# One attention stream over all pairs of heads, chain ends emitted a step later, and query maxima entered as rows by DMA

## The chip, the core and the metric

One core of a Trainium2 chip runs the whole program in one launch. The metric is device time in microseconds (us), the median of several executions. The engines named below are TensorE (PE in the profile; PEld is its weight load), VectorE (DVE), ScalarE (ACT), GpSimd (POOL) and the SP queue that issues most DMAs. Everything is float32.

## What is computed

The input is 16 images of 192 channels and 32x32 positions. Four residual layers follow, each `x = x + f(groupnorm(x))`; the change lies in layers 1 to 3.

```python
# layer 0: a recurrent block (mLSTM) plus a 3x3 convolution and batch norm over all images
# layer 1: 6 heads, 1024 tokens each; q and k (4 numbers a token) come from a small quantum circuit
scores = -(qn + kn - 2.0 * qk) / tau            # qk: product over 4 numbers
out = softmax(scores, axis=-1) @ v              # v: 32 channels of the head
# layer 2: deformable 3x3 depthwise convolution, 4 corners gathered for each tap
off = conv3x3(x, w_off) + b_off
acc = sum over 9 taps, 4 corners of gather(x, corner) * weight * w_def
# layer 3: 1x1 convolution, 2x2 Fourier weights, depthwise 3x3, gelu gate, 1x1 convolution
```

## The kernel before

`circuits` and `phase_a` (layer 0) come first and are not touched. `phase_b` runs layers 1 to 3 as four streams of Python generators, each going through the 16 images: `vectors` (layer 0's batch norm, x1, the group norm, the circuit's q and k), `attention`, `layer2` (`layer2_offsets`, then `layer2_gathers`) and `layer3`. Each `yield` names a cost; `weave` always goes on with the stream whose summed cost, divided by the stream's total for an image and shifted by its offset, is least. So one unit of `weave` is one image in each stream, and the offsets say how many images later a stream starts: 0, 1.1, 2.2, 3.5. The order so emitted is the order of preference in which the framework fills each engine's queue; an instruction whose inputs or buffer aren't there can be overtaken when that queue is laid out[...].

PSUM has eight banks: `big` (two buffers of two banks: `pmax`, `pscore`, `paug`, `pcirc`, `phad`), `mm` (two buffers of one bank: `pgn`, `pgv`, `pqub`, `ppsi`, `pz`, `pzt`, `pv`, `pxt`, `poffc`, `poff`, `pdt`, `pout`), `pav` and `pdef` (one each).

In `attention` heads go in pairs, three to an image. `largest(pr)` transposes the queries and keys of the pair (`rows_of`), makes all scores in 16 `pmax` products of 128 tokens by 512 keys for two heads, and takes their maxima on VectorE (L1139) into `mx`; the negative maximum then becomes column 5 of the query table `qp`. `values(pr)` transposes `qp` again with the maxima in it, and for each half of the tokens makes eight score products (`pscore`, L1160), each with an exponential on ScalarE (L1163), and their products with V (`pav`, L1170), two at a time right after the two exponentials. The sums are then copied, inverted by Ln and Exp (L1180, L1181) and multiplied (L1182). Between the steps of `values(pr)` stand those of `largest(pr + 1)`; `largest(0)` of an image stands alone, and the last pair has no maxima beside it.

In `layer2_gathers` a tap takes two gathers of 128 rows (L1311), corner 0 on ScalarE (L1298), three corners on VectorE (L1300), the tap's weight (L1316) and a product with the identity that sums taps in `pdef` (L1317); after nine taps the block is copied (`df`), transposed, added and stored. `layer3` ends with `pout` products, each followed at once by its addition and its store.

Of the kernel before, what the change touches and what calls it, by code (L numbers as in the profile page):

```python
# [19 lines left out]
HW = 1024  # L20
HS = 512


def groupstats(nc, pool, mm, cn, x):

    st = pool.tile([96, 2, 2, 6], F32, tag="gnst", name="gnst")
    mv = pool.tile([96, 2, 2], F32, tag="gnmv", name="gnmv")
    for k in range(2):
        for h in range(2):
            nc.vector.bn_stats(st[:, k, h, :], x[k][:, h * HS:(h + 1) * HS])  # L30
        nc.vector.bn_aggr(mv[:, k, :], st[:, k, :, :].rearrange("p a b -> p (a b)"))
    pg = mm("pgn")
    nc.tensor.matmul(pg[:96, 0:2], cn.g6, mv[:, :, 0], start=True, stop=True)
    gm = pool.tile([96, 2], F32, tag="gngm", name="gngm")
    nc.vector.tensor_copy(gm, pg[:96, 0:2])
    dd = pool.tile([96, 2], F32, tag="gndd", name="gndd")
    nc.vector.tensor_sub(dd, mv[:, :, 0], gm)
    nc.vector.tensor_mul(dd, dd, dd)
    nc.vector.tensor_add(dd, dd, mv[:, :, 1])
    pv = mm("pgv")  # L40
    nc.tensor.matmul(pv[:96, 0:2], cn.g6, dd, start=True, stop=True)
    rs = pool.tile([96, 2], F32, tag="gnrs", name="gnrs")
    nc.scalar.activation(rs, pv[:96, 0:2], AF.Ln, bias=cn.eps5[:96])
    nc.scalar.activation(rs, rs, AF.Exp, scale=-0.5)
    return gm, rs


def groupnorm(nc, pool, mm, cn, x, out):

    gm, rs = groupstats(nc, pool, mm, cn, x)  # L50
    nm = pool.tile([96, 2], F32, tag="gnnm", name="gnnm")
    nc.vector.scalar_tensor_tensor(nm, gm, -1.0, rs, ALU.mult, ALU.mult)
    for k in range(2):
# [718 lines left out]
def phase_b(tc, d, out, ydram, stats, cn, nb):  # L772

    nc = tc.nc
    with ExitStack() as ctx:
# [24 lines left out]
        def pairs(name):  # L800
            return p2.tile([128, 2, 192], F32, tag="acc", name=name, bufs=4)
# [97 lines left out]
        vo = p1.tile([128, 8, 3, 96], F32, name="vo")  # L899
        nc.vector.memset(vo[:, :, :, 32:64], 1.0)  # L900


        qp_, kp_, kt_, qt_ = [], [], [], []
        for i in range(2):
            for name, into, n in (("qp", qp_, 560), ("kp", kp_, 560), ("kt", kt_, HW), ("qt", qt_, HW)):
                if name == "kp" and i:
                    continue
                t = p1.tile([128, n], F32, name=f"{name}{i}")
                nc.gpsimd.memset(t, 0.0)
                into.append(t.rearrange("p (t c) -> p t c", t=8) if n == 560 else t)  # L910
# [10 lines left out]
        xnd = dp.tile([nb, 192, HW], F32, name="xnd")  # L921
        x1d, x2d, x3d = (dp.tile([nb, 192, HW], F32, name=f"x{i}d") for i in range(1, 4))
# [9 lines left out]
        def stream(i, work):  # L932
            for b in range(nb):
# [7 lines left out]
        weave([(stream(0, vectors), 86.0), (stream(1, attention), 189.6, 1.1), (stream(2, layer2), 144.5, 2.2),  # L941
               (stream(3, layer3), 121.4, 3.5)])


def vectors(g, b, left):
# [17 lines left out]
    groupnorm(nc, p2, mm, cn, x, xn)  # L963
    yield 8.0
# [52 lines left out]
    for pr in range(3):  # L1017
# [5 lines left out]
        psi = psi.rearrange("p t h a b -> p t (h a b)")  # L1023
# [7 lines left out]
        yield 4.0  # L1031
        prob = {}
        for w in range(2):
            for hf in range(2):
# [5 lines left out]
                prob[w, hf] = v4("prob")  # L1040
                nc.scalar.activation(prob[w, hf], pc, AF.Square)  # L1041
            yield 4.0

        pz = mm("pz")
        for hh in range(2):
            o = 20 - (pr * 2 + hh) * 4
            for w in range(2):
                for hf in range(2):
                    q = (w * 2 + hf) * 32
                    nc.tensor.matmul(pz[q:q + 32, :], g.amat[:, w, o:o + 32], prob[w, hf][:, hh * HS:(hh + 1) * HS],  # L1050
                                     start=(hh == 0), stop=(hh == 1))
# [4 lines left out]
        yield 4.0  # L1056
# [31 lines left out]
def attention(g, b, left):  # L1088

    nc, cn, p2 = g.nc, g.cn, g.p2  # L1090
    big, e4, row = g.big, g.e4, g.row
    qk, kr, vo = left.qk, left.kr, g.vo


    xn = [g.v4("xn")[:96] for _ in range(2)]
    for k in range(2):
        nc.sync.dma_start(xn[k], g.xnd[b, k * 96:k * 96 + 96, :])
    for t2 in range(4):
        pv = g.mm("pv")
        for j in range(2):  # L1100
            tt = t2 * 2 + j
            for k in range(2):
                nc.tensor.transpose(pv[:, (j * 2 + k) * 96:(j * 2 + k) * 96 + 96],
                                    xn[k][:, tt * 128:(tt + 1) * 128], cn.ident[:96, :96])
        for o in range(2):
            nc.scalar.activation(vo[:, t2 * 2:t2 * 2 + 2, :, o * 64:o * 64 + 32].rearrange("p a h e -> p (a h) e"),
                                 pv[:, 0:384].rearrange("p (a o e) -> p a o e", o=2, e=32)[:, :, o, :], AF.Copy,
                                 scale=row("gate"))
    yield 3.0
# [7 lines left out]
    def largest(pr):  # L1117

        qp, kp, kT, qT = g.qp_[pr % 2], g.kp_[0], g.kt_[pr % 2], g.qt_[0]
        for hh in range(2):  # L1120
            h, o = pr * 2 + hh, hh * 64
            nc.vector.tensor_copy(qp[:, :, o:o + 4], qk[:, :, 0, h, :])
            nc.vector.memset(qp[:, :, o + 4:o + 5], 1.0)
            nc.vector.memset(qp[:, :, o + 5:o + 6], 0.0)
            nc.vector.tensor_scalar_mul(kp[:, :, o:o + 4], qk[:, :, 1, h, :], g.rtau[:, 0:1])
            nc.vector.tensor_copy(kp[:, :, o + 4], kr[:, :, h])
            nc.vector.memset(kp[:, :, o + 5:o + 6], 1.0)
        rows_of(kp, kT)
        rows_of(qp, qT)
        yield 5.0  # L1130
        mx = p2.tile([128, 8, 2, 2], F32, tag="mx", name="mx")
        for tt in range(8):
            for hf in range(2):
                pm = big("pmax").rearrange("p (h s) -> p h s", h=2)
                for hh in range(2):
# [5 lines left out]
        nc.vector.tensor_tensor(qp.rearrange("p t c -> p c t")[:, 5::64, :].rearrange("p h t -> p t h"),  # L1141
                                mx[:, :, 0, :], mx[:, :, 1, :], ALU.min)

    att = g.xtile("att")

    def values(pr):

        kT, qT = g.kt_[pr % 2], g.qt_[1]
        rows_of(g.qp_[pr % 2], qT)
        for hf in range(2):  # L1150
            s = slice(hf * HS, (hf + 1) * HS)
            po = g.ps("pav")
            for t2 in range(4):
                pe = []
                for j in range(2):
                    tt = t2 * 2 + j
                    ps = big("pscore")
                    for hh in range(2):
                        r = slice(hh * 64, hh * 64 + 64)
                        nc.tensor.matmul(ps[:, hh * HS:(hh + 1) * HS], kT[r, tt * 128:(tt + 1) * 128], qT[r, s],  # L1160
                                         start=True, stop=True)
                    pe.append(e4("pexp"))
                    nc.scalar.activation(pe[j], ps, AF.Exp)  # L1163
                    if j == 0:
                        yield 1.2
                for j in range(2):
                    tt = t2 * 2 + j
                    for hh in range(2):

                        nc.tensor.matmul(po[hh * 64:hh * 64 + 64], vo[:, tt, pr, hh * 32:hh * 32 + 64],  # L1170
                                         pe[j][:, hh * HS:(hh + 1) * HS], start=(tt == 0), stop=(tt == 7))
                yield 3.3

            pc = p2.tile([128, HS], F32, tag="pavc", name="pavc", bufs=1)
            nc.scalar.activation(pc, po, AF.Identity)
            rd = p2.tile([128, HS], F32, tag="rd", name="rd", bufs=1)
            for hh in range(2):
                h = pr * 2 + hh
                num, den = (slice(0, 32), slice(32, 64)) if hh == 0 else (slice(96, 128), slice(64, 96))
                nc.scalar.activation(rd[num, :], pc[den], AF.Ln)  # L1180
                nc.scalar.activation(rd[num, :], rd[num, :], AF.Exp, scale=-1.0)  # L1181
                nc.vector.tensor_tensor(att[(h % 3) * 32:(h % 3) * 32 + 32, h // 3, s], pc[num], rd[num, :], ALU.mult)  # L1182
# [3 lines left out]
    for pr in range(3):  # L1186
        ahead = largest(pr + 1) if pr < 2 else iter(())
        for cost in values(pr):
            yield cost
            yield next(ahead, 0.0)  # L1190
        for cost in ahead:
            yield cost
    for k in range(2):
        x1 = g.v4("x1")[:96]
        nc.sync.dma_start(x1, g.x1d[b, k * 96:k * 96 + 96, :])
        nc.vector.tensor_add(att[:, k, :], att[:, k, :], x1)
        nc.sync.dma_start(g.x2d[b, k * 96:k * 96 + 96, :], att[:, k, :])
        yield 3.0
    left.x = att


def layer2(g, b, left):
    yield from layer2_offsets(g, b, left)
    yield from layer2_gathers(g, b, left)


def layer2_offsets(g, b, left):
# [5 lines left out]
    groupnorm(nc, p2, mm, cn, [x[:, k, :] for k in range(2)],  # L1213
              [xpad[:, k, 1:33, 1:33] for k in range(2)])
    yield 5.0
# [72 lines left out]
def layer2_gathers(g, b, left):  # L1288
# [3 lines left out]
    xg, ix, w4 = g.xg[b % 2], left.ix, left.w4  # L1292

    def corner(cr, part):
        for acc, j, gt, c in part:
            a, v, w = acc[:, j, :], gt[:, cr * 192:(cr + 1) * 192], w4[:, cr, c:c + 1]
            if cr == 0:
                nc.scalar.activation(a, v, AF.Copy, scale=w)  # L1298
            else:
                nc.vector.scalar_tensor_tensor(a, v, w, a, ALU.mult, ALU.add)  # L1300

    for hf in range(2):
        for j2 in range(2):
            po = g.ps("pdef")
            for t in range(9):
                part = []
# [290 lines left out]
```

## Time and profile before

| | us |
|---|---|
| median of 3 runs | 9228.33 |
| lowest and highest | 9214.2, 9228.97 |
| the profiled execution | 9226.07 |
| its span, first to last instruction | 9224.3 |

| engine | busy us | share | instructions |
|---|---|---|---|
| PE | 7894.4 | 86% | 30720 |
| DVE | 6946.3 | 75% | 14595 |
| ACT | 4251.9 | 46% | 7414 |
| POOL | 1882.9 | 20% | 1681 |

The mean granted TensorE clock is 0.909. A busy time counts instructions from start to end, waits not included. `phase_b` starts near 3332 us; from 4048 to 8481 all four streams run at once.

### The profile page before, as it was taken

To read this page: it belongs to the slowest core of one execution; us is meant where nothing else is said; L and a number is where in the kernel's file an instruction comes from. 1 tells how busy PE (TensorE), PEld (TensorE's weight loads), DVE (VectorE), ACT (ScalarE), POOL (GpSimd) and SP (SyncE) were. 2 spreads that over 40 slices of the span, in tenths; PEclk is the share of its full clock that TensorE was granted. 3 is DMA by queue.
4 is the path that set the end of the run, shared out by engine and by line. 5 is a ranking of instruction groups with operands and counts; after the bars stand their busy time and mean duration, and the time that the engine had idled before them with its cause. 6 is when DMAs were issued, how large, how long until landed. Compare 5 with 4: busy or idle time off the path is not lost. (4 is left out here: it accounts for less than half of the span.)

```text
span 9224.3 us, 92174 instructions
## 1 busy us (share of the span) xinstructions
PE 7894.4 (86%) x30720; PEld 3453.5 (37%) x30720; DVE 6946.3 (75%) x14595; ACT 4251.9 (46%) x7414; POOL 1882.9 (20%) x1681
## 2 busy tenths in 40 slices
PE   5999999999999969888888888888888888888853
PEld 2555555555555532233233233233233333333221
DVE  7777777777777743678878778878878878877887
ACT  3444444444454424444545545444544545445432
POOL 0100100100100100222312412322312322223341
PEclk9899999999999979998988998988988988989976
DMA  1111111111111120433433433433433333333341
GB/s 53 43 43 42 48 48 43 45 43 42 49 46 43 42 53 24 135 114 114 138 104 117 128 113 119 126 112 115 126 107 114 122 120 116 116 121 112 121 151 61
DMA packets 299050, 813.72 MB, mean 88 GB/s; under 512 B 46459, under 2 KB 162493, under 8 KB 298571
## 3 DMA queue, kind: packets, MB, share of 16 engines
q0 software_dynamic: 92160, 453.06, 15.9%
q1 hardware_dynamic: 206411, 354.76, 12.5%
q8 instruction: 241, 3.95, 0.2%
q14 instruction: 238, 1.95, 0.1%
HBM read 666.74 MB, written 132.54 MB: 87 GB/s over the span
## 5 line engine op out<-in xcount | busy, mean ns | idle before, releaser
L1311 POOL DMA_INDIRECT gt<-xg,ix x1152 | 1561.6, 1356 | 4173.2 <-DVE w L1283 1963.1
L1137 PE MATMUL pmax<-kt,qt 64*128 64x512 f32 x3072 | 1179.8, 724 | 316.2 <-DVE mx L1139 259.6
L1300 DVE SCALAR_TENSOR_TENSOR acc<-gt,w,acc 128x192 f32<-128x192 f32 x3456 | 1226.7, 410 | 292.9 <-ACT acc L1298 277.2
L1139 DVE TENSOR_REDUCE mx<-pmax 128x2 f32<-128x1024 f32 x768 | 934.2, 1217 | 415.1 <-PE pmax L1137 413.0
L1163 ACT ACTIVATE pexp<-pscore 128x1024 f32<-128x1024 f32 x768 | 776.6, 1018 | 799.1 <-PE pscore L1160 796.9
L1160 PE MATMUL pscore<-qt,kt 64*128 64x512 f32 x3072 | 991.3, 665 | 61.3 <-ACT prob L1041 28.6
L1170 PE MATMUL pav<-pexp,vo 128*64 128x512 f32 x3072 | 910.7, 649 | 137.1 <-ACT pexp L1163 136.3
L1298 ACT ACTIVATE acc<-gt,w 128x192 f32<-128x192 f32 x1152 | 482.8, 449 | 932.2 <-DMA gt<-xg,ix 550.1
L503 POOL COPY qbd<-qT 32x384 f32<-32x384 f32 x512 | 304.1, 594 | 2834.7 <-PE se L537 2749.9
L1417 DVE SCALAR_TENSOR_TENSOR dc<-pad,wdw,dc 128x512 f32<-128x512 f32 x1152 | 807.8, 742 | 10.8 <-ACT dc L1415 10.8
L1317 PE MATMUL pdef<-acc,ident 128*128 128x384 f32 x1152 | 576.4, 592 | 146.7 <-DVE acc L1316 141.0
L1137 PEld LDWEIGHTS pmax<-kt,qt 64*128 64x128 f32 x3072 | 336.4, 210 | 952.6 <-DVE mx L1139 491.5
L533 ACT ACTIVATE dm<-dm,wtm 128x128 f32<-128x128 f32 x1536 | 490.6, 388 | 348.2 <-DVE dm L489 268.1
L1160 PEld LDWEIGHTS pscore<-qt,kt 64*128 64x128 f32 x3072 | 306.5, 197 | 580.4 <-issue 385.9
L545 PEld LDWEIGHTS pintra<-v,pt 128*128 128x128 f32 x3072 | 425.2, 212 | 163.3 <-issue 71.7
L1170 PEld LDWEIGHTS pav<-pexp,vo 128*64 128x64 f32 x3072 | 163.5, 140 | 741.2 <-issue 402.8
L545 PE MATMUL pintra<-v,pt 128*128 128x33 f32 x3072 | 434.6, 290 | 2.5 <-DVE pt L540 2.4
L1317 PEld LDWEIGHTS pdef<-acc,ident 128*128 128x128 f32 x1152 | 201.5, 212 | 522.0 <-issue 249.5
L540 DVE SCALAR_TENSOR_TENSOR pt<-se,dm 128x512 f32<-128x512 f32 x384 | 262.5, 684 | 140.9 <-PE se L537 137.8
L537 PE MATMUL se<-qbd,kT 64*128 64x256 f32 x1536 | 290.6, 447 | 54.7 <-DVE pt L540 54.7
L1446 PE MATMUL pout<-gelu,wout 128*96 128x512 f32 x512 | 252.6, 631 | 80.8 <-DVE gelu L1440 80.8
L1316 DVE TENSOR_TENSOR acc<-acc,wdef 128x384 f32<-128x384 f32 x576 | 316.8, 550 | 2.7
(422 smaller groups left out, 12758.0 us busy)
## 6 DMA issues: line engine op xcount, KB each, us to landing
dm<-gd SPq DMA_DIRECT2D x128, 768.0 KB
xg<-xt SPq DMA_DIRECT2D x224, 192.0 KB
gt<-xg,ix POOLq DMA_INDIRECT x1152
xb<-x_in SPq DMA_DIRECT2D x32, 384.0 KB
y<-ydram SPq DMA_DIRECT2D x32, 384.0 KB
x1d<-xb SPq DMA_DIRECT2D x32, 384.0 KB
xnd<-y SPq DMA_DIRECT2D x32, 384.0 KB
xn<-xnd SPq DMA_DIRECT2D x32, 384.0 KB
```

Source lines behind the costliest of these rows:

```text
L533: nc.scalar.activation(dm[:, h, :], dm[:, h, :], AF.Exp, bias=wtm[:, c, 64 + h:65 + h])
L545: nc.tensor.matmul(pa[:, hh * 33:hh * 33 + 33], pt[:, h * 128:(h + 1) * 128], v33[:, hh, :], start=True, stop=True)
L1137: nc.tensor.matmul(pm[:, hh, :], qT[r, tt * 128:(tt + 1) * 128], kT[r, hf * HS:(hf + 1) * HS], start=True, stop=True)
L1139: nc.vector.tensor_reduce(mx[:, tt, hf, :], pm, AX.X, ALU.max, negate=True)
L1160: nc.tensor.matmul(ps[:, hh * HS:(hh + 1) * HS], kT[r, tt * 128:(tt + 1) * 128], qT[r, s], start=True, stop=True)
L1163: nc.scalar.activation(pe[j], ps, AF.Exp)
L1170: nc.tensor.matmul(po[hh * 64:hh * 64 + 64], vo[:, tt, pr, hh * 32:hh * 32 + 64], pe[j][:, hh * HS:(hh + 1) * HS], start=(tt == 0), stop=( ...
L1298: nc.scalar.activation(a, v, AF.Copy, scale=w)
L1300: nc.vector.scalar_tensor_tensor(a, v, w, a, ALU.mult, ALU.add)
L1311: nc.gpsimd.indirect_dma_start(out=gt, out_offset=None, in_=xg, in_offset=bass.IndirectOffsetOnAxis(ap=ix[:, c:c + 1], axis=0))
L1317: nc.tensor.matmul(po[:, 0:384], cn.ident, acc.rearrange("p j c -> p (j c)"), start=(t == 0), stop=(t == 8))
L1417: nc.vector.scalar_tensor_tensor(out, src, w, add, ALU.mult, ALU.add)
```

## The change

- `attention` becomes one generator over all 48 pairs of all images. `largest(i + 1)` stands between the steps of `values(i)` also from one image to the next. V of a pair is loaded and transposed in its `largest`; there are two query tables `qt`, one `qp`.
- The maxima leave `mx` by one transpose, a ScalarE copy and a DMA to DRAM (`mxd`), and come back as two rows of `qT`. The second `rows_of` and the constant columns' memsets go.
- `weigh` comes a step after its exponential; `sums` and `ends` of a half come in the first steps of the next half.
- `vectors`: one circuit product a step, `expect` a step later, the next pair's `products` before the last `expect`; `pz` is taken before the circuit products.
- `layer2_gathers`: gathers and corner 0 of a tap are emitted a tap ahead; a block's copy, transposes and store come in the next block or the next image. `layer2` is one stream over the images.
- `layer3` and the group norms: results are used a step after their products. `acc` has five buffers instead of four. Totals and offsets of `weave` follow.

```diff
 def groupstats(nc, pool, mm, cn, x):
...
+    yield 1.5
     pg = mm("pgn")
...
+    yield 1.5
     pv = mm("pgv")
     nc.tensor.matmul(pv[:96, 0:2], cn.g6, dd, start=True, stop=True)
+    yield 1.5
...
-        weave([(stream(0, vectors), 86.0), (stream(1, attention), 189.6, 1.1), (stream(2, layer2), 144.5, 2.2),
-               (stream(3, layer3), 121.4, 3.5)])
+        weave([(stream(0, vectors), 86.0), (attention(g), 205.8, 1.27), (layer2(g), 155.5, 2.49),
+               (stream(3, layer3), 131.9, 3.78)])
...
 def vectors(g, b, left):
...
+        pz = mm("pz")
+        ready = None
         for w in range(2):
             for hf in range(2):
...
-                prob[w, hf] = v4("prob")
-                nc.scalar.activation(prob[w, hf], pc, AF.Square)
-            yield 4.0
-        pz = mm("pz")
...
+                prob = v4("prob")
+                nc.scalar.activation(prob, pc, AF.Square)
+                yield 2.5
+                if ready:
+                    expect(*ready)
+                ready = w, hf, prob
+        if pr < 2:
+            psi = products(pr + 1)
+        yield 2.0
+        expect(*ready)
...
-def attention(g, b, left):
+def attention(g):
...
-    def largest(pr):
+    def largest(i):
...
+        xn = g.v4("xn")[:64]
+        nc.sync.dma_start(xn, g.xnd[b, pr * 64:pr * 64 + 64, :])
...
-            nc.vector.memset(qp[:, :, o + 4:o + 5], 1.0)
-            nc.vector.memset(qp[:, :, o + 5:o + 6], 0.0)
...
+        mq = p2.tile([128, 16], F32, tag="mq", name="mq")
+        nc.vector.tensor_tensor(mq.rearrange("p (h t) -> p t h", h=2), mx[:, :, 0, :], mx[:, :, 1, :], ALU.min)
+        pm = g.mm("pmq")
+        nc.tensor.transpose(pm[:16, 0:128], mq, cn.ident)
+        mr = p2.tile([16, 128], F32, tag="mr", name="mr")
+        nc.scalar.activation(mr, pm[:16, 0:128], AF.Identity)
+        nc.sync.dma_start(g.mxd[i].rearrange("h (t n) -> (h t) n", t=8), mr)
+        for hh in range(2):
+            nc.sync.dma_start(qT[hh * 64 + 5:hh * 64 + 6, :], g.mxd[i, hh:hh + 1, :])
+        yield 1.0
...
-    def values(pr):
-        kT, qT = g.kt_[pr % 2], g.qt_[1]
-        rows_of(g.qp_[pr % 2], qT)
+    def values(i):
...
+            last = None
+            for tt in range(8):
+                ps = big("pscore")
...
+                pe = e4("pexp")
+                nc.scalar.activation(pe, ps, AF.Exp)
+                yield 1.2
+                if tt == 0:
+                    todo.sums()
+                else:
+                    weigh(*last)
+                    if tt == 1:
+                        yield from todo.ends
+                last = tt, pe
+                yield 1.2
...
     yield from largest(0)
-    for pr in range(3):
-        ahead = largest(pr + 1) if pr < 2 else iter(())
-        for cost in values(pr):
+    for i in range(len(pairs)):
+        ahead = largest(i + 1) if i + 1 < len(pairs) else iter(())
+        for n, cost in enumerate(values(i)):
             yield cost
-            yield next(ahead, 0.0)
+            if n % 4 < 3:
+                yield next(ahead, 0.0)
...
-def layer2_gathers(g, b, left):
+def layer2_gathers(g, b, left, late):
...
+    coming = first(0)
+    for n, (block, t) in enumerate(taps):
+        (acc, part), coming = coming, first(n + 1) if n + 1 < len(taps) else None
...
+        if t == 0:
+            yield from late.tail
             po = g.ps("pdef")
...
+        if t == 8:
+            late.tail = tail(block, po)
...
 def layer3(g, b, left):
...
+            yield 1.5
+            total(m, slice(hf * HS, (hf + 1) * HS), po)
+            yield 0.5
```

## The prediction

> **What bounds the kernel now.** I read the page's busy rows first, then its slices, then busy time by stage, then the waits of the steady stage, then a timeline for what the totals can't show.
>
> The page's first part and its slices (busy tenths in 40 slices of 231 us):
>
> ```profile
> PE 7894.4 (86%) x30720; PEld 3453.5 (37%) x30720; DVE 6946.3 (75%) x14595; ACT 4251.9 (46%) x7414; POOL 1882.9 (20%) x1681
> ...
> PE   5999999999999969888888888888888888888853
> PEld 2555555555555532233233233233233333333221
> DVE  7777777777777743678878778878878878877887
> ```
>
> TensorE leads and VectorE follows; the part that the change touches begins in slice 15. Busy time by stage splits that part into ramp, steady and drain (columns: window, length, busy us of PE, PEld, DVE, ACT, POOL, granted clock, DMA share, GB/s). The cuts are the first ScalarE pass of `vectors` (3332), layer 3's first image (4048), `vectors`' last instruction (8481), and the end:
>
> ```profile
> 3332.00:4048.00 716.00, 602.72 (x2376) 213.47 (x2376) 366.65 (x740) 316.72 (x444) 79.85 (x74) 0.90 0.26 77
> 4048.00:8481.00 4433.00, 3829.94 (x13910) 1396.32 (x13912) 3554.04 (x7350) 2176.46 (x3386) 1247.44 (x928) 0.91 0.39 119
> 8481.00:9224.00 743.00, 456.15 (x1476) 179.44 (x1472) 608.78 (x1230) 280.30 (x464) 234.32 (x151) 0.78 0.36 109
> ```
>
> The steady stage holds 12.5 image periods (16 less layer 3's offset of 3.5), so 354.6 us each: PE busy 306, idle 48; DVE busy 284, idle 70. Neither engine is full; they wait for each other in turn. One period, by what attention is doing: `largest(0)` alone, pairs 0 and 1 with the next pair's maxima between, pair 2 alone:
>
> ```profile
> 5695.00:5755.00 60.00, 51.60 (x192) 22.32 (x192) 46.27 (x81) 19.03 (x33) 0.00 (x0) 0.77 0.22 65
> 5755.00:5984.00 229.00, 197.12 (x718) 65.88 (x714) 186.73 (x386) 114.74 (x172) 81.45 (x60) 0.94 0.41 124
> 5984.00:6047.00 63.00, 55.00 (x205) 22.10 (x204) 49.39 (x119) 38.43 (x64) 17.14 (x12) 0.93 0.48 148
> ```
>
> PE's busy share is level (0.86, 0.86, 0.87), so there is no large hole to fill. The clock is what differs: 0.77 against 0.94. Last, who waits in 4500 to 8500 (us in total, times, longest); the first group is PE's, the second VectorE's:
>
> ```profile
> PE pmax L1137 <- DVE mx L1139: 198.7, 121, 3.3
> PE pav L1170 <- ACT pexp L1163: 108.3, 100, 5.2
> PE pcirc L1039 <- DVE mx L1139: 28.4, 40, 1.3
> PE paug L1114 <- ACT pexp L1163: 27.2, 16, 2.8
> PE pscore L1160 <- ACT prob L1041: 22.1, 11, 2.4
> PE paug L1114 <- DVE qp L1141: 19.0, 11, 1.7
> ...
> PE pv L1103 <- ACT vo L1106: 14.2, 11, 2.5
> ```
>
> ```profile
> DVE mx L1139 <- PE pmax L1137: 219.0, 121, 6.3
> DVE acc L1300 <- ACT acc L1298: 204.2, 114, 16.2
> DVE att L1182 <- ACT rd L1181: 132.8, 48, 6.9
> DVE pad L1378 <- ACT low L1375: 65.2, 35, 5.5
> DVE psi L1020 <- PE pz L1050: 44.9, 11, 4.1
> ```
>
> The window holds 11.3 periods. PE's idle is ends of chains (a product right after its exponential) and the two `big` PSUM buffers, which VectorE frees late because it stood waiting for ScalarE.
>
> **The change, part by part** (us per image, minus is a gain; "step" is one score-sized unit of work).
>
> *Work.* Per pair, `rows_of` for the second query copy goes: 8 transposes (1.04 us as a group in the timeline) and one 1.01 us ScalarE copy, three times an image: PE -3.1, ACT -3.0. V's transposes go from 16 to 24, +1.0 at 0.13 each. New: a 128x16 transpose (nearest row: the 96x2 statistics matmuls, 0.33 for two) and a 16x128 ScalarE copy (between 0.20 and 0.37, the 96x2 and 128x96 rows; I take 0.25): PE +1.0, ACT +0.8. VectorE loses 18 memsets of 0.065: -1.2. PE net: -1.
>
> *Clock.* The 60 us stretch does 51.6 us of PE work at 0.77. Without a stretch of maxima alone, every window is like the second one above. At 0.94 that work takes 51.6 x 0.77 / 0.94 = 42, so -9.5. The Trainium skill ("TensorE: Matmul & The Clock Gate", section on HAM oscillation) puts a halved clock down to PE gaps over about 3.4 us. Here the longest wait PE had in that stretch was 2.3 us, with PE 86% busy, so by the rule nothing throttles there and rearranging gains 0; by the row -9.5. The measured clock decides that the loss exists, but not that it goes with the arrangement: the thin matmuls of `pqub` and the offsets, part of the same stretch, remain. I take -7.
>
> *Waits moved.* `weigh` now comes a whole step after its exponential: pav<-pexp 108.3/11.3 = -9.6. The second `rows_of` goes with its wait on qp (19.0) and half of paug<-pexp (13.6): -2.9. `pcirc` one per step in place of two: half of 22.1, -1.0. V's transposes no longer fill two `mm` banks in a row: 14.2, -1.2. Of VectorE's waits, acc (corner 0 a tap earlier), att (a step later), pad and psi are all taken on: 447/11.3 = 40 of its 70 idle us. That alone moves no end; it makes VectorE free `big` earlier. Of pmax<-mx and pcirc<-mx together, 227/11.3 = 20, I take half: -10. Sum -25. What is late next is again pmax<-mx, since every maximum still needs 1.22 us of VectorE for about 1.0 us of PE, and VectorE at 284 in some 330 us is 86% full. I give 8 back for that and the next two items: -17.
>
> *PSUM held longer.* `pz` is taken before the four circuit matmuls and freed after them, 12 of 86 cost units, three times: one of two `mm` banks is held 42% of the time. The skill's rule against this is "Evacuate promptly — 2 MiB is tight" ("PSUM — Partial Sum Buffer", its summary of rules). The waits for `mm` banks seen now (pv<-vo 14.2, pxt<-xt 12.8, poff<-ot 12.8) are 3.5 an image. By the rule they double or worse for that 42%, +1.5 or more; by the rows alone, 0 where the single bank is free in time. I count +1.5, inside the 8. Adding up the yields, `pz` and `poffc` (18 of 155.5 units) both stand when the second pair's `pmq` wants a bank; it can't start until the offsets end, some 14 us later. Instructions of one engine do overtake in this program (the timeline has two pscore records, then pav, then the other pscore records), so PE isn't stopped by that.
>
> *Queues.* SP gets ten issues an image more (one xn load, nine row transfers, about 0.3 each), 3 us in 330 of a queue that mostly waits. POOL's gathers move a tap ahead with corner 0, but `gt` keeps 6 buffers, so one tap fewer is in flight. ScalarE's corner 0 already waits 308.7 us for gathers in that window; each wait also holds the exponentials queued behind it. With `weigh` a step later that is covered; uncovered it would be up to the pav wait again, +9.6.
>
> *Rows by DMA.* ScalarE's copy, a write to DRAM, a read back into two rows. The nearest pair in the trace is a 24 KB write and its dependent read:
>
> ```profile
> 161.19 0.34 SPq L364 DMA_DIRECT2D gd<-gt  x1
> 162.78 0.81 SPq L487 DMA_DIRECT2D dm<-gd  x2
> ```
>
> VectorE got that read at 167.00, so 5.8 us for both, an upper bound as the read there is 768 KB; the lower is the write's 1.6 twice, 3.2. With transpose and copy: 3.8 to 6.4. By the yields the pair's first score follows the last maximum by 0.051 period, 17 us. Covered: 0. For the second pair the bank leaves 21 - 14 = 7 us: just covered.
>
> *Ends of the streams.* Offsets 1.1, 2.2, 3.5 become 1.27, 2.49, 3.78. The steady stage loses 0.28 period (-99). The others, at their measured rates: vectors alone 0.17 x 69 = 12; with attention 0.12 x 211 = 25; three streams -3; attention, layers 2 and 3 0.17 x 312 = 53; layers 2 and 3, 0.12 x 250 = 30; layer 3 -1. Net +17 for the run.
>
> *Sum.* Per steady image -1 - 7 - 17 = -25, times 12.22 = -305. In the 2.56 periods where attention runs beside layer 2 without all streams, 60% of that: -38. Ends +17. Total -326. The profiled execution took 9226.1 us (its span and 2 more), 2 below the median shown; 9226 - 326 = 8900.
>
> **The rivals.** *The waits come back.* Both engines stay coupled through two `big` buffers; VectorE's saved waits turn into mx<-pmax, the clock keeps its dips. Per image then -8 (pav's wait or the clock, not both): -98 - 10 + 17 gives 9135. For it: pmax<-mx is PE's largest wait and its buffers are unchanged. Against: two thirds of VectorE's idle loses its cause.
> *The rows come late (slower).* The two transfers stand in SP's order behind others that wait: x3d<-x waited 1101.3 us in 27 waits in that window, 41 us each. If the write of one pair an image is held that long, its first score is 41 + 6 - 17 = 30 us late, and TensorE's queue behind it: 16 x 30 = +480, on the 8938 of the steady part and ends alone: about 9420. It decides from some 11 us of hold (a second pair from 1). Against: what SP waits for is then itself the work of that moment, and the list order puts the write where its input is due.
> *It does less than it says.* Since instructions already overtake, "a step later" may be an order that the queue had. Then only work, rows and clock are left: -8, the first rival's number. The 108.3 us at pav speak against it.
>
> **How the numbers follow.** Forecast 0.70; back again or less than said 0.18 (most of it still faster, 0.03 of it within 0.2%); rows late 0.12, of which 0.03 at a price small enough to leave it faster. About 0.2% (18 us) is what can be told from no change. Best end: clock -9.5 and waits -35 without the 8 given back, about -46 an image, which would give 8620; I cut at 8690. Upper end 9170, past the first rival. Faster 0.88, same 0.03, slower 0.09.
>
> **What would show it.** Right: PE busy above 0.90 in the steady stage, pav<-pexp near nothing, acc<-acc and att<-rd under a third, no stretch with a clock under 0.85, a period near 330, the drain some 80 us longer. Wrong: a pscore row waiting for qt or a DMA (rows late); POOL or ScalarE's corner 0 waiting longer with DVE acc behind it; PE waiting for zr or ot (banks); a period above 345 with pmax<-mx grown.

## The result, and the profile after

The changed kernel takes 9212.1 us (median; 9191.0 to 9231.7), the kernel before 9228.7 in the same runs: ratio 0.9983, interval 0.9974 to 0.9992. That is 17 us less where the forecast said 328 less. The profiled execution has a span of 9199.0 us.

The page's first part and slices of the changed kernel:

```profile
PE 8010.2 (87%) x30512; PEld 3387.7 (37%) x30512; DVE 6945.0 (75%) x14313; ACT 4235.8 (46%) x7395; POOL 1784.4 (19%) x1680
...
PE   5999999999999969998998988988988898988853
...
DVE  6777777777777744668788778788788788778888
```

TensorE has 208 fewer matmuls and is busy 116 us longer. Its share in the slices rises as forecast; the time doesn't fall with it. Busy time by stage (columns as before: window, length, busy us of PE, PEld, DVE, ACT, POOL, clock, DMA share, GB/s; cuts at the same events), and under it the window 4500 to 8000 of the kernel before and of the changed one:

```profile
3345.00:4032.00 687.00, 601.78 (x2357) 205.94 (x2358) 369.73 (x688) 316.93 (x443) 83.68 (x72) 0.93 0.26 80
4032.00:8381.00 4349.00, 3878.01 (x13604) 1320.43 (x13606) 3482.83 (x6981) 2123.61 (x3311) 1112.58 (x900) 0.92 0.39 118
8381.00:9197.00 816.00, 511.09 (x1595) 189.46 (x1593) 675.41 (x1373) 317.08 (x521) 267.50 (x180) 0.75 0.37 115
```

```profile
4500.00:8000.00 3500.00, 3032.00 (x11040) 1112.07 (x11040) 2802.06 (x5794) 1717.23 (x2671) 956.40 (x716) 0.91 0.39 118
```

```profile
4500.00:8000.00 3500.00, 3122.40 (x10926) 1063.41 (x10926) 2815.02 (x5634) 1712.03 (x2655) 890.45 (x720) 0.92 0.39 118
```

The ends came out near the forecast, taken together: the ramp took 687 us, 29 less than before, where the forecast has some 15 more (34 for the ends, less 19 of gain), and the drain is about 75 longer, where it has some 63 (82 less 19). The steady stage did not: 4349 us over 12.22 periods is 356 each, not 330. The period itself, taken from here on as the mean spacing of `vectors`' last instruction over nine images, is 352.3 us before and 351.3 after. TensorE is busy 3032.00 / 3500 of it before, 305 us, with 47 idle; after, 313 busy with 38 idle. VectorE is busy 282 in both. So TensorE's idle time did fall, by 9, and its busy time rose by 8.

The waits of TensorE and of VectorE, 4500 to 8500 (us in total, times, longest):

```profile
PE pscore L1188 <- DVE mx L1151: 89.1, 37, 5.9
PE pmax L1149 <- ACT pexp L1191: 71.9, 53, 2.8
PE pmax L1149 <- DVE mx L1151: 35.7, 44, 1.5
PE paug L1115 <- ACT pexp L1191: 32.4, 14, 3.2
...
PE pav L1180 <- ACT pexp L1191: 26.7, 14, 3.9
```

```profile
DVE mx L1151 <- PE pmax L1149: 258.0, 142, 6.4
DVE pos L1315 <- PE poff L1310: 168.5, 11, 15.3
DVE pad L1450 <- ACT low L1445: 103.4, 35, 5.9
DVE acc L1387 <- ACT acc L1361: 97.2, 72, 3.6
DVE gngm L37 <- PE pgn L35: 55.5, 13, 6.1
DVE att L1220 <- ACT rd L1212: 18.6, 23, 4.2
```

Most waits that the change aims at shrank: pav behind its exponential from 108.3 to 26.7, acc from 204.2 to 97.2, att from 132.8 to 18.6, pmax behind mx from 198.7 to 35.7. Two grew: pad from 65.2 to 103.4, paug behind its exponential from 27.2 to 32.4. Others came in their place: maxima now wait for exponentials and scores for `mx`, and VectorE waits some 15 us an image for layer 2's offsets (pos), which was not among its waits before. Added up over all of TensorE's rows, the waits for exponentials went from 13.5 to 12.6 us an image, those for `mx` from 20.0 to 11.4. Four stretches of 35 us of one period show how uneven it is:

```profile
5293.00:5328.00 35.00, 28.98 (x97) 10.61 (x95) 33.27 (x69) 21.55 (x33) 10.22 (x10) 1.00 0.42 123
...
5363.00:5398.00 35.00, 27.81 (x71) 8.43 (x72) 31.43 (x53) 12.96 (x16) 0.00 (x0) 0.76 0.12 34
5398.00:5433.00 35.00, 33.63 (x150) 9.97 (x148) 27.61 (x43) 20.23 (x26) 0.00 (x0) 1.00 0.41 123
5433.00:5468.00 35.00, 34.80 (x143) 9.41 (x141) 14.46 (x36) 12.70 (x17) 7.56 (x8) 1.00 0.30 95
```

In the first VectorE is nearly full and TensorE is not; in the last TensorE is full and VectorE is busy for 14 of 35 us. And the clock still falls to 0.76 in one of them, though no stretch of maxima alone is left.

One matmul group explains the rise of TensorE's busy time. The same window for the instructions on `pz` alone, in the kernel before, the changed one, and `a_four` (below):

```profile
4500.00:8000.00 3500.00, 78.49 (x480) 14.87 (x480) 13.76 (x20) 6.87 (x10) 0.91 0.39 118
```

```profile
4500.00:8000.00 3500.00, 228.56 (x476) 42.86 (x476) 13.03 (x19) 6.91 (x10) 0.92 0.39 118
```

```profile
4500.00:8000.00 3500.00, 57.71 (x480) 12.52 (x480) 13.48 (x20) 6.92 (x10) 0.90 0.39 118
```

As many matmuls, each 0.59 us long in all three, but their union is three times as long: 23 us an image for 8. Before, the 16 of a pair stand together and the four column groups of `pz` overlap; in the change they come four at a time, between circuits, one column group at a time, and hardly overlap.

### The profile page after: what moved, and what is told of

Same layout as the page of the kernel before. It is cut to its first block, busy times and chain, and to the rows that moved or that the text cites. A ratio compares the mean times of both kernels' runs of the same rounds, so it can differ in the third digit from the quotient of the medians.

```text
span 9199.0 us, 91391 instructions
## 1 busy us (share of the span) xinstructions
PE 8010.2 (87%) x30512; PEld 3387.7 (37%) x30512; DVE 6945.0 (75%) x14313; ACT 4235.8 (46%) x7395; POOL 1784.4 (19%) x1680
## 5 line engine op out<-in xcount | busy, mean ns | idle before, releaser
L1357 POOL DMA_INDIRECT gt<-xg,ix x1152 | 1463.8, 1271 | 4235.7 <-DMA xn<-xnd 1165.5
L1149 PE MATMUL pmax<-kt,qt 64*128 64x512 f32 x3072 | 1097.0, 671 | 174.2 <-ACT pexp L1191 83.6
L1188 PE MATMUL pscore<-qt,kt 64*128 64x512 f32 x3072 | 1017.7, 690 | 196.7 <-DVE mx L1151 109.7
L1180 PE MATMUL pav<-pexp,vo 128*64 128x512 f32 x3072 | 962.4, 658 | 80.9 <-ACT pexp L1191 57.2
L1393 PE MATMUL pdef<-acc,ident 128*128 128x384 f32 x1152 | 597.3, 604 | 125.4 <-DVE acc L1389 111.1
L1149 PEld LDWEIGHTS pmax<-kt,qt 64*128 64x128 f32 x3072 | 315.6, 197 | 757.8 <-issue 202.1
L1188 PEld LDWEIGHTS pscore<-qt,kt 64*128 64x128 f32 x3072 | 286.5, 201 | 712.2 <-issue 300.8
L1049 PE MATMUL pz<-prob,amat 128*32 128x512 f32 x768 | 366.5, 603 | 0.9 <-ACT prob L1061 0.9
L1061 ACT ACTIVATE prob<-pcirc 128x1024 f32<-128x1024 f32 x192 | 195.6, 1020 | 351.3 <-PE pcirc L1059 344.8
```

The lines of the kernel that those rows point to most:

```text
L1149: nc.tensor.matmul(pm[:, hh, :], qT[r, tt * 128:(tt + 1) * 128], kT[r, hf * HS:(hf + 1) * HS], start=True, stop=True)
L1180: nc.tensor.matmul(po[0][hh * 64:hh * 64 + 64], vo[:, tt, hh * 32:hh * 32 + 64], pe[:, hh * HS:(hh + 1) * HS], start=(tt == 0), stop=(tt = ...
L1357: nc.gpsimd.indirect_dma_start(out=gt, out_offset=None, in_=xg, in_offset=bass.IndirectOffsetOnAxis(ap=ix[:, c:c + 1], axis=0))
L1393: nc.tensor.matmul(po[:, 0:384], cn.ident, acc.rearrange("p j c -> p (j c)"), start=(t == 0), stop=(t == 8))
```

## The experiments

All edits are small. Three theories are named in the expectations: A, the lost overlap of `pz`; W, VectorE's wait for the offsets; P, that it matters which stages of the four images in flight coincide, which the three start offsets in `weave` decide (called starts below; layer 2's own offsets are another thing). Ratios are to the kernel before, run on the same chip.

### Theory A, and the rows by DMA

`b_serial` is the kernel before, with the loops around the `pz` matmuls turned so that one column group follows another.

```
# shortened
-for hh: for w: for hf:  matmul(pz[q:q + 32, :], ...)
+for w: for hf: for hh:  matmul(pz[q:q + 32, :], ...)
```

> The kernel before, with one edit: the 16 matmuls of pz for a pair are issued one column group after another (loops w, hf, hh in place of hh, w, hf). Same instructions, same place in the stream. Theory A (the four column groups of pz no longer overlap; the trace after shows 0.463 us a record where before has 0.159): pz takes 22 us of TensorE an image in place of 7.7, and the kernel becomes slower by 8 to 14 us an image, 100 to 220 us in all, about 9330 to 9450. Theory B (the gain was lost because TensorE-heavy parts of the streams now coincide, offsets, circuits and pout): the order inside pz matters little here, 9230 to 9260.

0.9996 (0.9983 to 1.0009). `pz` is busy 87.61 us in the window, for 78.49: the 16 still overlap, so this was no test of A. The next three are. `a_four` is the changed kernel with the four products of a pair first and then its 16 matmuls together; `a_pairs` sends them two column groups at a time; `a_four_rows` is `a_four` with the maxima going into the queries by a second transposition, as before.

```
# shortened
-    if ready: expect(*ready)      # 4 matmuls behind each product
-    ready = w, hf, prob
+    ready.append((w, hf, prob))
+yield 2.0
+pz = mm("pz"); expect(ready)      # 16 matmuls together
```

> The changed kernel, with pz made as before: all four circuit products first, then the 16 matmuls over four column groups together, then the next pair's products. Theory A: pz falls from 22 to about 8 us an image and 8 to 14 us an image come back: 9000 to 9110. Theory B: 9180 to 9220, with VectorE's wait for the offsets' transposes (168 us in 4500 to 8500) still there. The late use of the products (psi waiting for pz) should come back with 4 us of VectorE an image in either case.

> The changed kernel, with the two halves of one circuit taken together, so two of the four column groups overlap, a step after their squares. Theory A: pz at about 11 us an image (half of 22) and about two thirds of the gain of four together, 9030 to 9140, or as good as four together if the step's delay is worth anything. Theory B: 9190 to 9220.

> The changed kernel with pz as before, and the maxima entered by transposing the query table a second time at the end of largest (8 transposes, one 1.0 us copy a pair) in place of the two rows by DMA. If the rows by DMA cost nothing hidden, this is 3 to 6 us an image slower than the same kernel with DMA rows (40 to 90 us). If the DMA chain holds up first scores or blocks SP (SP waits 359 us for mr in 4500 to 8500), it is faster than it.

| kernel | us | ratio | interval |
|---|---|---|---|
| a_four | 9172.8 | 0.9941 | 0.9925 to 0.9958 |
| a_pairs | 9206.2 | 0.9976 | 0.9967 to 0.9986 |
| a_four_rows | 9172.7 | 0.9933 | 0.9917 to 0.9950 |

A is worth some 40 us, not 310. The window 4500 to 8000 of `a_four`:

```profile
4500.00:8000.00 3500.00, 2994.18 (x10909) 1051.00 (x10906) 2805.69 (x5615) 1705.89 (x2650) 923.63 (x716) 0.90 0.39 118
```

TensorE is busy 301 us a period, 12 less than after the change, and idle 51, 13 more; the period stays at 352.0. In the steady stage the time of the lost overlap had stood in TensorE's idle time. The gain was made before it: `vectors` ends its first image 23 us earlier than in the changed kernel, and layer 3 starts its first 36 us earlier. The rows by DMA cost and gain nothing that these runs can tell.

### Theories W and P

`a_four_pos` is `a_four` with the cost of VectorE's `pos` work put ahead of it (`yield 6.0` moved up). `a_phase` is the changed kernel with two numbers changed, `a_four_phase` the same on `a_four`, and `a_four_image` is `a_four` with the attention image by image again, at the starts of the kernel before.

```
-(layer2(g), 155.5, 2.49), (stream(3, layer3), 131.9, 3.78)
+(layer2(g), 155.5, 2.89), (stream(3, layer3), 131.9, 4.2)
```

> The changed kernel with pz made as before, and in layer2_offsets the 6.0 of cost put between the transposes of the offsets and VectorE's work on them, in place of behind it. Theory W (a wait moved: VectorE's queue stands 13.5 us an image at pos for TensorE's poff, 134.9 us in 4500 to 8000, and that took the place of the waits removed): the wait falls under 3 us and about 8 us an image come back, 9172 to about 9070. Theory P (stages of the streams that need TensorE coincide with one another, and so do those that need VectorE; the order inside one chain matters little): the wait turns up elsewhere, 9150 to 9200.

> The changed kernel as it is, with the offsets of weave alone changed to 2.89 and 4.2. Theory P: a gain like that of the same shift with pz as before, less what pz costs: 9212 to about 9100. If pz's 14 us of TensorE now fall where VectorE is full, the two kernels come out alike; if the shift gains nothing here, P is not the cause.

> The changed kernel with pz made as before, and only the offsets of weave changed: layer 2 at 2.89 in place of 2.49, layer 3 at 4.2 in place of 3.78. The offsets' products then no longer stand beside the second pair's circuits and layer 3's pout. Theory P: adding up each stream's TensorE and VectorE work by weave time, the sum over windows of the greater of the two falls by some 13 us an image (339 to 326); the ends cost 0.42 image more, some 30 us; so 9172 - 11.8 x 13 + 30, about 9050 (9000 to 9120), with the period near 340. Theory W: the pos wait goes too as TensorE isn't full there, 9060 to 9110. If neither holds, the longer ends alone are seen: 9200.

> The changed kernel with pz made as before, but attention again image by image: the first pair's maxima of an image stand alone, and the offsets of weave are those of before (1.1, 2.2, 3.5). Everything else stays: products a step later, rows by DMA, corner 0 a tap ahead. Theory P: the stretch of maxima alone (VectorE work) stood beside the offsets (TensorE work) and was their counterweight; bringing it back gives the removed waits their worth, 9000 to 9120. If the endless stream is itself a gain that something else ate, this is slower than 9172: 9200 to 9280.

| kernel | us | ratio | interval |
|---|---|---|---|
| a_four_pos | 9175.2 | 0.9946 | 0.9929 to 0.9963 |
| a_phase | 9051.6 | 0.9816 | 0.9803 to 0.9829 |
| a_four_phase | 9101.2 | 0.9862 | 0.9848 to 0.9876 |
| a_four_image | 9064.3 | 0.9827 | 0.9815 to 0.9840 |

`a_four_pos` is inconclusive: the wait on poff stayed at 134.9 us, so the edit didn't move it. `a_phase` gives 160 us for two numbers, in spite of more ramp and with `pz` as spread as ever; `a_four_phase` gives 72 on `a_four` and lies in the range that P had. P's main claim holds. `a_four_image` doesn't single out a cause, since it changes the starts too.

### How far theory P can forecast

For P I had added up, over one period, the larger of TensorE's and VectorE's load, each instruction placed by its stream's costs. Four kernels test that sum: `b_shift` and `b_good` are the kernel before with layers 2 and 3 at 2.6 and 3.9, and at 3.0 and 4.3; `a_phase_m` and `a_phase_2` are the changed kernel with attention, layer 2 and layer 3 at 1.27, 2.64, 3.93 and at 1.45, 2.95, 4.38.

> The kernel before with one edit: layers 2 and 3 start 0.4 images later (2.6 and 3.9 for 2.2 and 3.5). Theory P (the time is set by which stages of the four images in flight coincide; the old offsets were good, since layer 2's matmul-heavy offsets lay beside VectorE's `largest` of head 0): the sum over one period of the larger of TensorE's and VectorE's load rises from 331 to 345 us an image, so +14 x 12 = some +165 us, and 0.4 images of ramp: 9380 to 9430 us. Rival (phases matter only since the change made the attention a stream): only the ramp of some 0.4 x 85 us at most, 9230 to 9265 us.

> The kernel before with one edit: layers 2 and 3 start 0.8 images later (3.0 and 4.3 for 2.2 and 3.5). It tells how much of the gain of the changed kernel with other offsets (9052 us) comes of offsets alone. Theory P: the load sum falls from 331 to 319 us an image, so some -145 us and up to +60 us of ramp: 9030 to 9150 us. Rival (the old attention gains nothing from phases, since its chains of waits hold each period): 9228 us or up to 60 us above it. If it comes under 9080 us, the change itself is worth nothing at equal phases; if it stays over 9150 us, the change is worth at least 1%.

> The changed kernel with layers 2 and 3 0.15 images later (2.64 and 3.93 for 2.49 and 3.78), where 0.4 later gave 9052 us. Theory P: the load sum is 340 us an image against 339, so no gain: 9200 to 9235 us. Rival (any later start helps in proportion, since buffers of the rows before are free by then): 0.15/0.4 of the 160 us, 9150 us.

> The changed kernel with offsets 1.45, 2.95 and 4.38 for 1.27, 2.49 and 3.78. Theory P: the load sum is the lowest found, 319 us an image, for 325 at 2.89 and 4.2 (9052 us): some 60 us less in the steady stage and up to 40 us more of ramp, 8970 to 9040 us. Rival (a later start is what helps, and costs ramp beyond what it gives): 9060 to 9110 us.

| kernel | us | ratio | interval |
|---|---|---|---|
| b_shift | 9543.3 | 1.0342 | 1.0311 to 1.0372 |
| b_good | 9205.7 | 0.9967 | 0.9952 to 0.9982 |
| a_phase_m | 9058.3 | 0.9800 | 0.9779 to 0.9821 |
| a_phase_2 | 9055.7 | 0.9797 | 0.9777 to 0.9817 |

The starts rule the kernel before as well, so the rival that only a stream of pairs is touched falls. But the forecasts miss all four, `b_shift` by over 100 us and `a_phase_m` by over 140, with no gain foretold and the whole gain measured. The periods say where. In the kernel before the sum was near: 16.4 us longer for the 14 forecast in `b_shift`, 12.0 shorter for 12 in `b_good`, and what is missing lies in ramp and drain, which by an estimate took back some 115 us in `b_good` (12.0 for each of 11.7 periods, less the 23 gained) where 60 was allowed. In the changed kernel the sum itself fails: 13 shorter for 1 longer in `a_phase_m`, and `a_phase_2` 4 above `a_phase` where 6 below was forecast. P holds as a statement on what matters, not as a model of it.

### Which stream

`a_l2` moves layer 2 alone by 0.15 images, `a_l3` layer 3 alone, `a_half` both by 0.07; `b_m` moves both by 0.15 in the kernel before.

```
a_l2:   2.49, 3.78 -> 2.64, 3.78        a_half: 2.49, 3.78 -> 2.56, 3.85
a_l3:   2.49, 3.78 -> 2.49, 3.93        b_m:    2.2, 3.5   -> 2.35, 3.65
```

> The changed kernel with layer 2 alone 0.15 images later (2.64 for 2.49; layer 3 stays at 3.78). Theory L2 (the offset convolutions of layer 2 stand beside the circuits of the vectors and VectorE waits 15 us an image for them): 9050 to 9100 us, and `pos <- poff` gone. Theory L3 (layer 3's place against the attention decides): 9190 to 9230 us. If only the two together act: 9120 to 9190 us.

> The changed kernel with layer 3 alone 0.15 images later (3.93 for 3.78; layer 2 stays at 2.49). Theory L2: 9190 to 9240 us, with `pos <- poff` at about 15 us an image still. Theory L3: 9050 to 9100 us.

> The changed kernel with layers 2 and 3 0.07 images later (2.56 and 3.85), half of the shift that gave 9058 us. If the wait for the offsets fades in proportion: about 9135 us. If it is one instruction that falls on one side or the other of a queue: either 9060 or 9210 us.

> The kernel before with layers 2 and 3 0.15 images later (2.35 and 3.65 for 2.2 and 3.5). At 0.4 later it took 9543 us and at 0.8 later 9206 us. Theory that the change itself is worth some 1.7% at good offsets: nothing near here goes under 9180 us, and with the offset convolutions moving towards the circuits it is 9250 to 9400 us. Rival (the kernel before was in a bad place too, and 0.15 frees it): 9070 to 9150 us.

| kernel | us | ratio | interval |
|---|---|---|---|
| a_l2 | 9501.1 | 1.0284 | 1.0259 to 1.0309 |
| a_l3 | 8967.2 | 0.9716 | 0.9690 to 0.9742 |
| a_half | 9411.0 | 1.0204 | 1.0172 to 1.0235 |
| b_m | 9385.3 | 1.0170 | 1.0140 to 1.0199 |

Theory L2, and with it W, falls. In `a_l2` pos no longer waits for poff, and it is the slowest changed kernel; in `a_l3` the wait stays, and it is the fastest:

```profile
DVE pos L1315 <- PE poff L1310: 135.4, 12, 11.6
```

Theory L3 had the sign of `a_l3`, but would have left `a_l2` where it was, and no theory had 9411 for half of a shift of which the whole gives 9058. `b_m` lies in the range of its first theory. The time is jagged in these numbers, but not at every touch: the five edits inside one stream (`b_serial`, `a_pairs`, `a_four`, and `a_four_rows` and `a_four_pos` against `a_four`) moved it by 40 us at most. The shifts moved it by 72 to 315, `b_good` by 23. The windows 4500 to 8000 of `a_l3` and of `a_l2`:

```profile
4500.00:8000.00 3500.00, 3101.10 (x11446) 1073.93 (x11447) 2946.83 (x5927) 1817.33 (x2819) 1013.02 (x744) 0.95 0.41 123
```

```profile
4500.00:8000.00 3500.00, 3087.78 (x10235) 1048.27 (x10232) 2647.49 (x5326) 1632.97 (x2518) 945.49 (x680) 0.90 0.37 111
```

TensorE is busy for nearly the same share of the time, with 12% more matmuls done in `a_l3`. With each kernel's period:

| us per image | period | TensorE busy | idle | VectorE busy | clock |
|---|---|---|---|---|---|
| before | 352.3 | 305 | 47 | 282 | 0.91 |
| before, layer 3 later (`b_l3`, next) | 339.9 | 296 | 44 | 282 | 0.94 |
| b_m | 363.5 | 308 | 56 | 284 | 0.90 |
| b_shift | 368.7 | 314 | 54 | 280 | 0.89 |
| after | 351.3 | 313 | 38 | 282 | 0.92 |
| a_l3 | 334.5 | 296 | 38 | 282 | 0.95 |
| a_phase | 334.2 | 295 | 39 | 281 | 0.95 |
| a_phase_m | 338.3 | 299 | 40 | 282 | 0.95 |
| a_half | 369.9 | 324 | 46 | 282 | 0.91 |
| a_l2 | 373.0 | 329 | 44 | 282 | 0.90 |

The changed kernel's matmuls take TensorE between 295 and 329 us an image, and the period follows that; in the kernel before (296 to 314) idle time moves too (44 to 56). From after to `a_l3` idle time doesn't change at all; busy time falls by 17. Matmul time that starts while the granted clock is under 0.9 (it is 0.5 then, and a matmul of `pmax` takes a median of 1057 ns for 589) falls from 50.6 to 25.4 us an image. By an estimate those 25 us would take about half at full clock, so 11 to 13 of the 17 are the clock. For the slower kernels the clock explains less. In `a_l2` that time is 65.6 us, which makes some 7 of the 16 that TensorE is busier there than after the change; in `a_half` it is 57.2, some 3 of 10. In these two `pav` stands out: up to the next matmul's start its matmuls take 64.0 and 69.6 us an image, for 58.4 after the change, though at full clock each is as long (0.62 us on average). So they overlap less.

### What the change is worth where layer 3 stands well

`b_l3` is the kernel before with layer 3 alone 0.15 later (3.65 for 3.5). `a_four_l3` is `a_four` with layer 3 at 3.93.

> The kernel before with layer 3 alone 0.15 images later (3.65 for 3.5; layer 2 stays at 2.2). If the change itself is worth its 2 to 3% once the places of layers 2 and 3 suit, this kernel stays at 9200 to 9300 us. If the wider distance between layers 2 and 3 is all that helps, it gives the kernel before the same 260 us: 8960 to 9050 us.

> The changed kernel with layer 3 0.15 images later, and with the 16 matmuls of z emitted together after the four products as before the change. If the missing term is paid in full (14.5 us an image over 12.2 images): 8790 to 8830 us. If TensorE has that time free (VectorE the bound, or later starts of the next products): 8950 to 9010 us.

`b_l3` takes 9076.4 us, 0.9826 (0.9808 to 0.9845); `a_four_l3` takes 8951.0, 0.9698 (0.9671 to 0.9725), the lowest time here, though not to be told from `a_l3`. `b_l3` lies between its two forecasts: the shift alone gives the kernel before 1.7%, and the change at the same shift another 1.1%. `a_four_l3` is at the foot of its second forecast: TensorE is busy 284 us a period and idle 52, against 296 and 38 in `a_l3`. Again the spread `pz` takes only idle time.

So at equal shifts of layers 2 and 3 the changed kernel against the one before, in per cent of the latter's unshifted time, and the difference in TensorE's busy and idle time, us an image (4500 to 8000):

| moved later by | kernel before | changed kernel | difference | busy | idle |
|---|---|---|---|---|---|
| 0, 0 | 0 | -0.2 | -0.2 | +8 | -9 |
| 0, 0.15 | -1.7 | -2.8 | -1.1 | 0 | -6 |
| 0.15, 0.15 | +1.7 | -2.0 | -3.7 | -9 | -16 |
| 0.4, 0.4 (changed: 0.4, 0.42) | +3.4 | -1.8 | -5.3 | -19 | -16 |

The shifts count from each kernel's own starts, so the rows are four draws and not four equal places. The change gains in each; how much, the row decides, and of the four the starts it came with gain least. Idle time falls in every row, twice by about the 17 that the forecast took for waits; busy time, forecast to fall by 8, runs from 8 more to 19 less.

## Why the prediction was wrong

**The step that failed** is the pricing of the starts. "Ends of the streams" costs 1.27, 2.49, 3.78 for 1.1, 2.2, 3.5 at +17 us, for the lengths of ramp, steady stage and drain alone. That was near for ramp and drain together (+46 for some +78), but the same three numbers also decide what stands beside what in the steady stage, and there the prediction put them at nothing, without a reason. Two of them move the changed kernel between 8967 and 9501 us and the kernel before between 9076 and 9543; the changed kernel's period moves 17 us down and 22 up. The forecast of -25 an image measured -1. A period near the forecast's 330 (334.5) came only with layer 3 moved. What led to it is the reading of the profile: "PE's busy share is level (0.86, 0.86, 0.87), so there is no large hole to fill", and from it that every window would look like the second one. Level busy shares over 60 to 229 us hid that a busy TensorE is not TensorE at its pace, and shorter stretches of the kernel before were less level, 0.81 to 0.99 for TensorE over ten stretches of 35 us:

```profile
5353.00:5388.00 35.00, 30.79 (x93) 12.89 (x89) 26.97 (x44) 2.51 (x5) 0.00 (x0) 0.70 0.02 6
...
5458.00:5493.00 35.00, 34.53 (x105) 11.74 (x104) 25.30 (x59) 12.38 (x22) 13.98 (x13) 0.98 0.54 172
```

No rival had this mechanism either; none of their numbers was drawn from moving a stream.

**Work, -1 an image: wrong by the `pz` term.** I counted instructions and left out that a matmul moved away from its neighbours loses their overlap: +15 us of TensorE (366.5 us on the page for 127.2, over 16 images). In the steady stage it is paid in idle time: taking it back leaves the period (352.0 for 351.3; 336.0 for 334.5). It accounts for the 40 us of `a_four` at most.

**Clock, -7: right that it goes with the arrangement, wrong that this arrangement brings it.** Matmul time at the lower clock went from 58.1 to 50.6 us an image, by the same estimate worth about -3.8. In `a_l3` it is 25.4, worth -16 against before. I had weighed the skill's rule of gaps over 3.4 us against the row and followed the row; that the clock falls without such gaps holds (last section).

**Waits, -25 and 8 given back: some went, the wait for exponentials moved.** pav behind pexp lost 7.2 us an image of the 9.6 forecast, but maxima came to wait for the exponentials in its place, so all of TensorE's waits for them fell by 1.0. Those for `mx` fell by 8.6, near the 10 that I took. TensorE's idle time fell by 9 only, and in `a_four`, where spread `pz` matmuls don't fill it, it rose by 4, to 51. At these starts what the moved steps freed came back as other waits.

**PSUM held longer, inside the 8:** the three waits for `mm` banks that the prediction names (pv, pxt, poff) are no longer among TensorE's; that they would double was my own estimate, the rule it quotes has no size. **Rows by DMA, 0: supported** by `a_four_rows`. SP's wait at the write to DRAM fits:

```profile
SPq L1160 <- ACT mr L1159: 359.1, 24, 20.5
```

SP stands there for ScalarE's copy, so in these 24 of some 34 transfers the queue was ready first, and no row of TensorE's waits names a DMA. The slow rival, 9420 us by late rows, did not happen; "the waits come back" was nearest, 9135, with the right idea on waits and clock, the wrong size, and nothing on the starts.

**The signs named beforehand:** att fell under a third (18.6 of 132.8) and the drain grew as forecast; acc (97.2 of 204.2) and pav (26.7 of 108.3) fell, but not so far; TensorE's share came to 0.89, not above 0.90, stretches under clock 0.85 remained, and the period was over 345, though without more pmax behind mx. So most local steps could be seen to work while their sum did not arrive.

What stays open is why layer 3's place matters as it does: the runs show that the clock and the overlap of matmuls, and so TensorE's busy time, change with it, but which collision lets the clock fall, or whether gaps come first and the clock second, was not separated. VectorE's wait for layer 2's offsets does not decide it: `a_l3` keeps that wait, `a_l2` loses it. Not run either: the changed kernel as it is at the starts of before, and a shift of attention's start alone.

## What to carry to other kernels

When a change moves the relative starts of interleaved streams, treat the starts as an edit of their own: 0.07 to 0.4 of a period moved this kernel by up to 3% either way, more than the change that came with them. Compare two structures at several equal shifts, or the verdict is one on the shift. Before pricing a schedule, split an engine's time into busy and idle per period: where busy time for the same matmuls differs between arrangements, look at the clock and at the overlap of matmuls, not at the waits alone.

## What the hardware showed that was not expected

- Matmuls on `pz` overlap in a burst and hardly when spread. In `a_four` four of them start within 0.02 us and the next four 0.45 later, 0.59 us long each. `pz` takes 7.7 us an image in one burst of 16, 8.6 with the order turned, 11.2 two groups at a time and 22.1 one group at a time (matmul time up to the next matmul's start, 4500 to 8000). That the overlap is one between column groups is inferred from the program; the records don't name the group.
- The clock is lowered after gaps of some 2 us as well. The Trainium skill ("TensorE: Matmul & The Clock Gate", HAM oscillation) speaks of gaps over about 3.4 us. Before the change there were 89 stretches of lowered clock between 4500 and 8000, 640 us in all; in the 12 us ahead of them TensorE had a gap over 3.4 us in 6 cases and one over 2 us in 70, or 79%. Ahead of moments of full clock, taken every 0.5 us, 21% have one over 2 us. In `a_l2`, the slowest changed kernel, 50 of 74 had a gap over 3.4. So the lowered clock goes with long gaps, and with gaps of some 2 us too; that the gap is the trigger is inferred from order in time.
